# A four-layer graph network on one core: layer 0's second dense layer turned, graph 0 aggregated by rows, a bias put in PSUM by ScalarE, and other numbers for the planner

## The chip, the core and the metric

The kernel runs on one core of one Trainium2 chip. The metric is device time in microseconds for one execution on all 32 graphs. TensorE (PE in the profile) multiplies matrices and writes to the accumulator memory PSUM (8 banks of 512 fp32 columns on 128 partitions); PEld is its loading of stationary operands. VectorE (DVE) and ScalarE (ACT) do the elementwise work, GpSimd (POOL) a few powers, and SyncE (SP) issues every DMA. All data are fp32.

## The reference, cut to what matters

For each of 32 graphs there are 512 nodes with 256 features, `x`, and a dense 512 x 512 adjacency `adj`. Four layers run one after the other; each ends in a layer norm without affine.

```
layer 0: h = (1 + eps) * x + adj @ x;  x = LN(x + relu(h @ W1 + b1) @ W2 + b2)       (W1: 256x512, W2: 512x256)
layer 1: h = adj @ (x @ W.T + b);      x = LN(x + where(h > 0, h, alpha * h))        (W: 256x256)
layer 2: n = LN(x) * gamma + beta;     x = LN(x + x + relu((adj @ n) @ W_rel + b_rel + n @ W_root))
layer 3: h = (epsilon * x + adj @ x) @ W1 + b1;  h = silu(rmsnorm(h) * w)
         x = LN(x + h @ W2 + b2)                                                     (W1: 256x1024, W2: 1024x256)
```

Layer 1's bias goes through the aggregation, so in the kernel it becomes `b_1` times the row sum of the adjacency for each node.

## The kernel before, in words

**Tiling.** `x` of a graph lies in one tile of 128 partitions x 1024 columns (four chunks of 128 nodes, 256 features each), called a room; there are 36 rooms of that size. The adjacency comes as four chunks of 128 x 512, with rows and columns exchanged, in two rooms. An aggregate gives `aT`, features on partitions, nodes in columns (2 x 512).

**Seven products.** Nearly every matrix product is done as 2 x 2 blocks with seven products instead of eight (`seven`, line 800): sums of blocks are made on DVE (`left_sums`, `right_sums`), seven products go to three PSUM banks, and each result is copied (`take`) or added (`put`) to its block. An aggregate (`aggregate`, line 916) has 7 x 2 matmuls of 256 columns. To add the self-loop `1 + eps` or `epsilon`, the diagonal blocks of the adjacency and of two of its sums get a multiple of the identity (`with_loops`); layer 0 keeps the old diagonals in DRAM (graph 0: in a room) and `restore` (line 887) brings them back for layer 1.

**Dense layers.** `dense_feat` (line 956) gives its result with features on partitions and 256 columns to a matmul. The second dense layers come in two forms. `dense_add` (line 1009) has features of the tokens as output: for each product and each 128-row piece of the contraction two matmuls of 128 columns, and DVE adds each of seven results to `x` directly. `dense_turned` (line 1034) exchanges the operands: one matmul of 256 columns in place of two of 128; the results lie features first, so that ACT evicts four of them with the bias per partition, DVE adds three, DVE transposes 32 x 32 squares (two instructions), four DMAs put the squares into a DRAM tile `corner`, one DMA reads it back (`spread_squares`, line 1214), and `add_turned` (line 1073) adds the result to `x` in two halves. `TURN` (line 119) says for which graphs a layer is turned: `TURN[layer][0] < graph < B - TURN[layer][1]`. Before, only layer 3 is turned, for graphs 1 to 28. Where layer 0 isn't, `plus_row` adds its bias `b2_0` to `x` (two DVE instructions).

**Layer 1.** `dense_tok` (line 944) computes a half (256 nodes x 256 features) with four matmuls in one PSUM bank. Lines 1319 to 1327: DVE adds bias times row sum out of PSUM into `v` (two instructions a half), ACT makes `relu(-v)`, DVE the rest.

**Norms.** `Norm.half` sums each chunk and its squares on ACT (an activation and a read of its accumulator each); POOL raises the variance to -0.5; `put` (line 1149 ff.) scales a chunk on DVE or ACT, whichever the planner takes. The last two graphs (`HALVES`) are normed in two halves, with statistics on DVE, and go out by half.

**The order of the work.** The whole program is first recorded as operations with their inputs and outputs, each with a cost in microseconds for each engine that can do it. `Plan.order` (line 443) then plays them through a model of the five engines, DMA included, and writes the order out; the hardware runs exactly that order on each engine's queue. Up to 5 graphs are in flight. An operation's rank is its due time: `graph * period + need`, with `RULES` = (period, pace, spacing of the last three graphs, near) and `SHIFT` moving single graphs. `YIELD` is a penalty in microseconds for giving DVE a step that ACT can do as well. `wire_time`, `ADVANCE`, `AFTER`, `SPARE` and `KEEP` model transfers. Line 337 is a helper that issues every recorded instruction, so nearly all rows of the profile have that line and are told apart by their tiles: `ps` is PSUM, `room` a working tile, `few` small columns, `A` the sums of weight blocks, `L_gnn_W` a weight (digits left out).

**Start.** Nine warm-up matmuls on zeros (line 1405) run while the first graph is loaded; then layer 0 of graph 0 makes the sums of the adjacency, copies four diagonals on ACT, adds the loops and aggregates by seven products.

Of the kernel before, what the change touches and what calls it, by code (L numbers as in the profile page):

```python
# [14 lines left out]
P = 128  # L15
# [16 lines left out]
def matmul_time(n):  # L32
    return (0.224 if n <= 128 else 0.432), 0.163
# [34 lines left out]
ISSUE, ADVANCE, AFTER, LANES = dict(sync=0.48, within=0.66, gpsimd=1.5), 1.5, 0.4, 8  # L68
# [3 lines left out]
SPARE = 1.0  # L72
# [3 lines left out]
def wire_time(kbytes):  # L76
    return kbytes / 385


# [20 lines left out]
YIELD = 1.6  # L100
# [8 lines left out]
RULES = [(34, 1.8, 11, 0.4)]  # L109
# [3 lines left out]
SHIFT = {-1: -21, 1: 3, 2: 6}  # L113


AHEAD, LAST = 85.0, 500.0


TURN = {0: (99, 0), 2: (99, 0), 3: (0, 3)}
HALVES = 2  # L120


class Pool:
# [7 lines left out]
    def clear(self):  # L131
        self.halves = [None] * (2 * len(self.tiles))

# [18 lines left out]
    def take(self, room):  # L152
        whole, halves = self.free()
        if room.whole or not halves or whole and whole[0][0] < halves[0][0] - 1.0:
            room.index = whole[0][1]
        else:
            room.index = halves[0][1]
# [4 lines left out]
class Room:  # L162
# [3 lines left out]
    def __init__(self, pool, whole=True):  # L166
        self.pool, self.whole = pool, whole
# [65 lines left out]
class Op:  # L233
# [8 lines left out]
    kbytes: float  # L242
# [9 lines left out]
class Plan:  # L252
# [29 lines left out]
    def add(self, ways, out, ins, ordered=None, port=False, kbytes=0, late=0.0, crosses=False):  # L282
        me = len(self.ops)
        op = Op(self.graph, ways, port, crosses, "scalar" in ways, kbytes, late)
# [28 lines left out]
    def do(self, out, *ways, ordered=None, scrap=None):  # L313


        ins = []
# [29 lines left out]

    def row(self, steps):
# [21 lines left out]
    def move(self, out, src, kbytes, engine="sync", late=0.0, into=None, outof=(), issue=None, **kw):  # L369


        within = engine == "sync" and isinstance(out, Part) and isinstance(src, Part)
        kind = "within" if within else engine

        def put():
# [4 lines left out]
            {engine: ((issue or ISSUE[kind], ADVANCE + late + wire_time(kbytes) + AFTER + KEEP), put)},  # L380
            into or out, [*outof, *([src] if isinstance(src, Part) else [])],
            kbytes=kbytes, late=late,
# [60 lines left out]
    def order(self, period, pace, last, near):  # L443
# [28 lines left out]
        while can_start:  # L472
# [19 lines left out]
            def rooms_free(op):  # L492
# [7 lines left out]
                for r in first:  # L500
# [6 lines left out]
                    if not r.whole and k < len(halves):  # L507
                        taken[pool, False] = k + 1
                        at = max(at, halves[k][0])
                        continue  # L510
                    n = taken.get((pool, True), 0)
# [11 lines left out]
            for i in can_start:  # L523
# [7 lines left out]
                if op.kbytes and "sync" in op.ways:  # L531
                    wait = max(wait, lanes[0])
# [4 lines left out]
                    at, key=lambda e: at[e] + sum(op.ways[e][0]) + YIELD * (op.yields and e == "vector")  # L537
# [31 lines left out]
            if op.kbytes:  # L569
                wire = max(wire, t + ADVANCE) + wire_time(op.kbytes)  # L570
                end = wire + op.late + AFTER + SPARE
# [928 lines left out]
```

## Time and profile before

| what | us |
|---|---|
| median of 3 runs (lowest, highest) | 2285.55 (2285.33, 2286.13) |
| the profiled execution | 2285.65 |
| its span, first to last instruction | 2283.9 |
| first matmul on data / end of the last matmul | 9.59 / 2272.8 |

The mean granted TensorE clock is 0.999. The chain of work that ended last goes, in its last part, over ScalarE's rows at 2273.37 and 2277.90. Groups of instructions that the change touches, over the whole run:

| engine | what | count | mean ns |
|---|---|---|---|
| PE | matmul records, stationary `room`, moving `A`, 128 columns | 1728 | 275 |
| PE | matmul records, stationary `room`, moving `L_gnn_W`, 128 columns | 1280 | 275 |
| DVE | `room <- ps, room`, 256 columns | 944 | 416 |
| ACT | `room <- ps, L_gnn_b_c`, 256 columns (eviction with bias) | 880 | 469 |
| DVE | `room <- L_gnn_b, few, ps`, 256 columns (layer 1's bias) | 128 | 472 |
| DVE | `room <- room, L_gnn_b`, 512 columns (`plus_row`) | 72 | 686 |
| SP | `corner <- room`, 128 KB, issue to landing 2.6 us | 232 | |
| SP | `room <- corner`, 512 KB, issue to landing 3.7 us | 28 | |

How to read it: a row of the timeline has start, length, engine, line, operation, tiles written and read, shape and count, and in brackets the idle time before it with what ended it. A row of windows has the stretch, then each engine's busy time with its number of instructions, then the granted clock, the busy share of the DMA engines and GB/s. An fp32 matmul leaves two records. A record's length includes the pipeline, so that neighbours overlap: what a matmul costs in a full stream is the distance between starts.

### The profile page before, as it was taken

The numbers are of one execution on the slowest core, as the hardware profiler recorded it, in microseconds if no ns is written. First come the engines' busy times: TensorE is split into PE (matmuls) and PEld (weight loads), VectorE is DVE, ScalarE is ACT, GpSimd is POOL, SyncE is SP. The second block draws the span as 40 slices with busy tenths as digits, with TensorE's granted clock in tenths as the row PEclk, the third lists the DMA queues.
The fourth block names the chain that finished last, engine by engine and source line by source line (L and its number), as shares of the span: only waits on it lengthen the run. The fifth ranks groups of instructions, "written<-read, shape, count | busy, mean of one in ns | idle before, by whom it ended". The sixth has DMA issues, their size and how long they took to land. (4 is left out here: it accounts for less than half of the span.)

```text
span 2283.9 us, 38000 instructions
## 1 busy us (share of the span) xinstructions
PE 2268.7 (99%) x12434; PEld 2044.5 (90%) x12434; DVE 2132.9 (93%) x5471; ACT 1693.8 (74%) x4551; POOL 241.1 (11%) x168
## 2 busy tenths in 40 slices
PE   9999999999999999999999999999999999999998
PEld 8999998999988999889999899998899988988987
DVE  8999999999999999999999999999999999989898
ACT  4776677777787777777777877778777777778686
POOL 0001110111101111101111011110111101101010
PEclk9999999999999999999999999999999999999999
DMA  7102122323222232222222232322223232232201
GB/s 245 27 21 70 46 66 57 93 74 89 70 63 77 74 93 66 83 56 84 84 74 77 54 91 77 83 73 65 77 75 93 65 84 56 75 79 59 68 10 65
DMA packets 244582, 167.71 MB, mean 73 GB/s; under 512 B 141856, under 2 KB 207648, under 8 KB 244384
## 3 DMA queue, kind: packets, MB, share of 16 engines
q1 hardware_dynamic: 244384, 165.29, 25.7%
q8 instruction: 98, 1.61, 0.3%
q14 instruction: 100, 0.82, 0.1%
HBM read 109.33 MB, written 55.37 MB: 72 GB/s over the span
## 5 line engine op out<-in xcount | busy, mean ns | idle before, releaser
L337 PE MATMUL ps<-room,room 128*128 128x256 f32 x3584 | 940.9, 380 | 1.6 <-DMA room<-in_x_dram 1.2
L337 DVE TENSOR_TENSOR room<-room,room 128x512 f32<-128x512 f32 (+1 forms) x1416 | 811.6, 598 | 6.5 <-ACT room L337 1.4
L337 PEld LDWEIGHTS ps<-room,room 128*128 128x128 f32 x3584 | 651.1, 190 | 77.8 <-DVE room L337 1.8
L337 PE MATMUL ps<-room,L_gnn_W 128*128 128x256 f32 x2432 | 654.4, 380 | 1.4 <-DVE room L337 1.1
L337 DVE TENSOR_TENSOR room<-ps,room 128x256 f32<-128x256 f32 (+1 forms) x1232 | 568.2, 479 | 85.2 <-PE ps L337 78.2
L337 PE MATMUL ps<-room,A 128*128 128x256 f32 x1824 | 509.2, 380 | 0.0
L337 PEld LDWEIGHTS ps<-room,L_gnn_W 128*128 128x128 f32 x2432 | 444.4, 190 | 54.2 <-DVE room L337 1.9
L337 ACT ACTIVATE room<-ps,L_gnn_b_c 128x256 f32<-128x256 f32 x880 | 364.6, 469 | 161.4 <-PE ps L337 161.0
L337 POOL TENSOR_TENSOR few<-few,mhalf 128x4 f32<-128x4 f32 (+3 forms) x162 | 240.4, 1486 | 2035.0 <-DVE few L337 1786.0
L337 ACT ACTIVATE room<-room,few 128x256 f32<-128x256 f32 x635 | 335.0, 591 | 60.8 <-DVE few L337 60.6
L337 PEld LDWEIGHTS ps<-room,A 128*128 128x128 f32 x1824 | 326.1, 191 | 35.4 <-ACT room L337 0.9
L337 PE MATMUL ps<-L_gnn_W,room 128*128 128x128 f32 (+1 forms) x1792 | 344.4, 305 | 0.0
L337 ACT ACTIVATE scrap<-room,few 128x256 f32<-128x256 f32 x500 | 250.6, 502 | 107.8 <-DVE few L337 106.7
L337 PEld LDWEIGHTS ps<-L_gnn_W,room 128*128 128x128 f32 x1792 | 291.2, 191 | 28.4
L337 DVE TENSOR_TENSOR room<-room 128x256 f32<-128x256 f32 (+1 forms) x640 | 307.7, 495 | 4.4 <-ACT room L337 1.9
L337 ACT ACTIVATE room<-ps 128x256 f32<-128x256 f32 (+1 forms) x516 | 194.2, 378 | 153.5 <-PE ps L337 147.4
L337 PEld LDWEIGHTS ps<-A,room 128*128 128x128 f32 x1728 | 258.8, 191 | 17.7
L337 PE MATMUL ps<-A,room 128*128 128x128 f32 x1728 | 272.8, 275 | 0.0
L337 ACT ACTIVATE room<-room 128x1024 f32<-128x1024 f32 (+2 forms) x260 | 243.5, 939 | 28.1 <-DVE room L337 20.3
L337 ACT ACTIVATE scrap<-room 128x256 f32<-128x256 f32 x500 | 204.7, 412 | 51.4 <-DVE room L337 44.7
L337 ACT ACTIVATE room<-room,L_gnn_rms_weight_c 128x512 f32<-128x512 f32 x256 | 176.4, 719 | 22.0 <-DVE room L337 18.9
L337 DVE TENSOR_TENSOR room<-room,loop 128x256 f32<-128x256 f32 x256 | 105.6, 415 | 7.4 <-PE ps L337 6.5
(60 smaller groups left out, 1163.3 us busy)
## 6 DMA issues: line engine op xcount, KB each, us to landing
room<-in_adj_dram SPq DMA_DIRECT2D x128, 256.0 KB, 5.0
corner<-room SPq DMA_DIRECT2D x232, 128.0 KB, 2.6
room<-in_x_dram SPq DMA_DIRECT2D x31, 512.0 KB, 6.4
room<-corner SPq DMA_DIRECT2D x120, 128.0 KB, 2.7
out_dram<-room SPq DMA_DIRECT2D x30, 512.0 KB, 3.0
room<-corner SPq DMA_DIRECT2D x28, 512.0 KB, 3.7
diagonal<-room SPq DMA_DIRECT2D x62, 128.0 KB, 1.8
room<-in_adj_dram SPq DMA_DIRECT2D x124, 64.0 KB, 2.0
```

Of the source, the lines that this page charges most:

```text
L337: getattr(getattr(self.nc, engine), method)(to, *(put(x) for x in args), **kw)
```

## The change

- `TURN[0]` goes from (99, 0) to (2, 3): layer 0's second dense layer is turned for graphs 3 to 28; `b2c_0` is added by ACT's eviction instead of `plus_row`.
- `aggregate_first` is new, for layer 0 of graph 0: no sums of blocks, but plain rows. As each chunk of the adjacency is there, its diagonal block gets the loop and two matmuls of 512 columns add up in two full PSUM banks; the diagonal is then read again from the input. The block sums are made afterwards, for the later layers. The four diagonal copies and their moves back go.
- In layer 1 ACT writes `b_1` times the row sum into the PSUM bank, after the whole of `aT` is there (`behind=[aT]`), and all matmuls of that half add to it (none is marked as first). Relu and the last step read PSUM. The pool of banks notes how many columns the last matmuls of a bank covered (`summed`), gives the seed a bank with all 512 covered, and prefers for other uses the bank with the fewest.
- The planner's transfer model has a pair of numbers for each kind of transfer; `ADVANCE` 1.5 to 1.0 (with `AFTER` gone), `SPARE` 1.0 to 0.8, `YIELD` 1.6 to 0.8, `RULES`, `SHIFT` and `AHEAD` have other values. `ONTO` and `PLAIN` are empty, so the code that they switch does nothing.

```diff
-ISSUE, ADVANCE, AFTER, LANES = dict(sync=0.48, within=0.66, gpsimd=1.5), 1.5, 0.4, 8
-SPARE = 1.0
+ISSUE, ADVANCE, LANES = dict(sync=0.48, within=0.66, gpsimd=1.5), 1.0, 8
+SPARE = 0.8
...
-def wire_time(kbytes):
-    return kbytes / 385
+def moving(kbytes):
+    return 0.1 + kbytes / 450, 1.0
+LOAD, LOAD_X, BLOCK = (0.76, 2.15), (1.68, 1.7), (0.31, 0.66)
+CORNER, PIECES = (0.42, 0.95), (0.54, 1.16)
+TURNED, QUARTER = (1.66, 1.02), (0.7, 0.8)
...
-YIELD = 1.6
+YIELD = 0.8
...
-RULES = [(34, 1.8, 11, 0.4)]
-SHIFT = {-1: -21, 1: 3, 2: 6}
-AHEAD, LAST = 85.0, 500.0
-TURN = {0: (99, 0), 2: (99, 0), 3: (0, 3)}
+RULES = [(35, 1.7, 14, 0.2)]
+SHIFT = {-1: -21, 1: 3, 2: 5, 5: 3, 6: -1, 11: 1, 27: 1, 29: 2, 30: -3}
+AHEAD, LAST = 89.0, 500.0
+TURN = {0:(2,3),2:(99,0),3:(0,3)}
+PLAIN = 0
+ONTO = ()
+SEED = 1
+BEHINDS = 1
...
+    def fit(self, room, whole):
+        return [w for w in whole if self.summed[w[1] // 2] >= room.onto]
...
+        if self.psum:
+            whole = self.fit(room, whole)
+            ready = [w for w in whole if w[0] <= now + 1e-9]
+            i = min(ready, key=lambda w: (self.summed[w[1] // 2], w))[1] if ready else whole[0][1]
+            room.index = i
+            self.summed[i // 2] = max(self.summed[i // 2], room.sums) if room.onto else room.sums
...
-    def dense_tok(steps, h):
-        ps = bank(HC, D)
+    def dense_tok(steps, h, start=None):
+        ps = bank(HC, D, onto=start is not None)
+        if start is not None:
+            for i in range(HC):
+                start(ps[:, i, :], h * HC + i)
...
-                    n == 0 and i == 0, n == len(steps) - 1,
+                    n == 0 and i == 0 and start is None, n == len(steps) - 1,
...
+    def aggregate_first(x, adjacency):
+        aT, ps = room(DC, N), [bank(N) for _ in range(DC)]
+        for m in range(NC):
+            chunk = adjacency.chunk(m)
+            own = chunk[:, m * P : (m + 1) * P]
+            add(own, own, loop0)
+            for k in range(DC):
+                mm(ps[k], x[:, m, k * P : (k + 1) * P], chunk, m == 0, m == NC - 1)
+            block = a["adj"][plan.graph][:, m, m * P : (m + 1) * P]
+            plan.move(own, block, BLOCK)
+        for k in range(DC):
+            for h in range(2):
+                copy(aT[:, k, h * TH : (h + 1) * TH], ps[k][:, h * TH : (h + 1) * TH])
+        adjacency.sums()
+        return aT
...
     def layer0(x, adjacency):
-        adjacency.sums()
-        adjacency.with_loops(loop0)
-        aT = aggregate(x, adjacency)
-        adjacency.restore()
+        if plan.graph:
+            adjacency.sums()
+            adjacency.keep()
+            adjacency.with_loops(loop0)
+            aT = aggregate(x, adjacency)
+            adjacency.restore()
+        else:
+            aT = aggregate_first(x, adjacency)
...
-            ps = dense_tok([(aT[:, k, :], W_1[:, k, :]) for k in range(DC)], h)
-            for i in range(HC):
-                c = h * HC + i
-                stt(v[:, c, :], b_1, rs[:, c : c + 1], ps[:, i, :], ALU.mult, ALU.add)
-            act(half(neg, h), half(v, h), AF.Relu, scale=-1.0)
+            if SEED:
+                ps = dense_tok(
+                    [(aT[:, k, :], W_1[:, k, :]) for k in range(DC)], h,
+                    lambda o, c: plan.do(o, scalar(AF.Copy, D, b_1, scale=rs[:, c : c + 1]), behind=[aT] if BEHINDS else []),
+                )
+                got = ps
...
+            act(half(neg, h), got, AF.Relu, scale=-1.0)
             stt(half(x, h), half(neg, h), nalpha, half(x, h), ALU.mult, ALU.add)
-            stt(half(v, h), half(v, h), 0.0, half(x, h), ALU.max, ALU.add)
+            stt(half(v, h), got, 0.0, half(x, h), ALU.max, ALU.add)
```

## The prediction, made before the changed kernel ran

> **What bounds the kernel now.** I read the page first, then the busy time by windows, the timeline of TensorE's records, and the two ends of the timeline.
>
> ```profile
> span 2283.9 us, 38000 instructions
> PE 2268.7 (99%) x12434; PEld 2044.5 (90%) x12434; DVE 2132.9 (93%) x5471; ACT 1693.8 (74%) x4551; POOL 241.1 (11%) x168
> ```
>
> A busy PE need not be a PE at its peak, since records overlap. So I take the distance from one record's start to the next row's start, in the steady middle:
>
> ```profile
> 1006.46 2.75 PE L337 MATMUL ps<-room,L_gnn_W 128*128 128x256 f32 x12
> 1009.05 1.03 PE L337 MATMUL ps<-room,A 128*128 128x256 f32 x4
> ...
> 1034.25 1.05 PE L337 MATMUL ps<-L_gnn_W,room 128*128 128x128 f32 x8
> 1035.14 0.60 PE L337 MATMUL ps<-room,A 128*128 128x256 f32 x2
> ```
>
> Twelve records of 256 columns take 2.59 us, 216 ns each; eight of 128 take 0.89 us, 111.4 ns as a mean over the trace. Every fp32 matmul is two such records. The program has 8,360 of the first kind after the 18 warm-up ones and 4,056 of the second: 8,360 x 0.216 + 4,056 x 0.1114 = 2,257.6 us. They run from 9.59 to 2,272.8 us, 2,263.2 us. So all idle time of TensorE in between is 5.6 us (2.0 before 25 us, 0.7 by 70 us, 2.7 after 1,890 us). Windows, columns us, PE, PEld, DVE, ACT, POOL:
>
> ```profile
> 9.00:25.00 16.00, 14.14 (x63) 11.68 (x64) 15.86 (x40) 4.70 (x12) 0.00 (x0) 1.00 0.95 308
> 350.00:1890.00 1540.00, 1540.00 (x8318) 1388.53 (x8317) 1445.91 (x3678) 1170.18 (x3148) 165.95 (x110) 1.00 0.27 76
> 2030.00:2273.00 243.00, 242.34 (x1445) 219.79 (x1443) 225.50 (x559) 171.65 (x451) 26.93 (x18) 1.00 0.16 43
> ```
>
> For 1,540 us nothing but TensorE's own work sets the time, at 94% DVE and 76% ACT. Only three things can shorten the run: fewer or cheaper matmuls, an earlier start, a shorter tail behind the last matmul. The two ends:
>
> ```profile
> 7.18 2.62 SPq L377 DMA_DIRECT2D room<-in_adj_dram  x4
> ...
> 9.59 5.42 PE L337 MATMUL ps<-room,room 128*128 128x256 f32 x24 [1.22 <-DMA room<-in_x_dram]
> 14.84 1.03 PE L337 MATMUL ps<-room,L_gnn_W 128*128 128x256 f32 x4
> 16.98 1.13 PE L337 MATMUL ps<-room,L_gnn_W 128*128 128x256 f32 x4 [1.11 <-DVE room L337]
> ```
> ```profile
> 2273.37 6.49 ACT L337 ACTIVATE room<-room,few 128x256 f32<-128x256 f32 x13
> ...
> 2274.49 5.99 SPq L377 DMA_DIRECT2D out_dram<-room  x6
> ...
> 2276.83 1.05 DVE L337 TENSOR_SCALAR room<-room,few 128x256 f32<-128x256 f32 x3
> ```
>
> At the start PE waits for x. At the end the last four graphs' 16 output rows come together; ACT scales 13 of them until 2,279.86 while DVE, given 3, is done at 2,277.88. The tail behind the last matmul is 11.1 us.
>
> **What the Trainium skill says.** "TensorE: Matmul & The Clock Gate", section "Back-to-back issue gap", gives columns / 2.4 + about 2.5 ns for a warm matmul. Two cycles a column fit the fp32 records here: 512/2.4 = 213.3, measured 216.0 (2.7 over); 256/2.4 = 106.7, measured 111.4 (4.7 over, more than the page). So two narrow records cost 6.8 ns more than a wide one. "PSUM — Partial Sum Buffer", section "The four PSUM rules", says that writes of ScalarE leave the bits alone which make a matmul add rather than overwrite; so the seed must go to a bank whose last matmuls covered all 512 columns. No trace of before shows a seed. "ScalarE: Activation LUTs", section "What ACT_TABLE_LOAD costs", adds about 93 ns for a per-partition pointer; the rows agree: 412 ns with none, 502 with one, 591 with two.
>
> **The change part by part.**
>
> *Turned layer 0, graphs 3 to 28 (26 graphs).* Out go 7 x 4 matmuls of 128 columns (56 records), in come 7 x 2 of 256 (28 records): 56 x 0.1114 - 28 x 0.216 = 0.190 us a graph, 26 x 0.190 = **4.95 us off the path**. DVE loses 7 adds of 0.416 and two bias adds of 0.686 (4.28), gains 3 adds of 0.416, two transposes of 0.698 and two adds of 0.682 (4.01): 0.27 less. ACT gains 4 evictions with bias of 0.469: 1.88. SP gains five DMAs a graph, 130 in all; four issues of this kind took 1.78 us and the read-back's 0.34, 2.1 us a graph. SP mostly waits (721 us on DVE alone), so its queue holds this. Latency: transposes 1.4, issues 2, landings 2.6 and 3.7, about 10 us before the norm; other graphs' matmuls hide it, as they hide the same path of layer 3 now (no PE idle in 1,540 us). If that cover were gone, every microsecond bared would cost 26 us.
>
> *Seed, all 32 graphs.* DVE loses 4 x 0.472 = 1.89 us a graph. ACT gains 4 copies with one pointer; into PSUM this form is not in the trace. Bounds: 0.41 (no pointer) to 0.59 (two); I take 0.50, so 2.0 us. The relu and the max-add then read PSUM at their present prices (0.62; 0.68). In steady state DVE goes from 65.7 to 63.5 us of 69.8 a graph, ACT from 53.2 to 57.1 (82%): neither passes TensorE. TensorE runs the same matmuls, but the first of each half now waits for two seeds on ACT, and each seed waits for the whole aggregate. Behind a waiting seed on ACT stand copies out of PSUM that free banks. The order has other graphs' matmuls ahead, so I price it at 0; range 0 to 0.3 us per half, 64 halves, for the slow rival; below zero it cannot be, as there is no idle to remove.
>
> *Graph 0 by rows.* 28 records of 0.216 (6.05 us) become 16 of 512 columns. That form is not in the trace: 0.429 by the page's formula (an estimate), at most 2 x 0.216; I take 0.430: 6.88, **0.83 us added**. But the first matmul needs one adjacency chunk and one x half instead of two chunks, sums and an x half which stands fifth in the queue. The warm-up records hold PE until 8.2, so the start moves from 9.59 to about 8.3, **1.3 off** (0.5 if x stays behind all four chunks in SP's order, as it lands near 8.8 now). Then aT is finished in one go and its first half is copied under the last two matmuls; of the 2.0 us idle before 25 us I take 0.7 off (bounds: 2.0 off, 1.0 added, as all copies fall due together). Four 0.42 us ACT copies and four SP moves go, four diagonal re-reads of 64 KB (2.0 us landing) and four short DVE adds come; all finish under layer 0's dense matmuls. Start together: 0.83 - 1.3 - 0.7 = **-1.2** (from -2.5 to +0.5).
>
> *Order.* New margins, shifts, last graphs spaced 14 apart instead of 11, and the penalty for giving a shared step to DVE halved to 0.8. Nothing to gain in the middle, where idle is zero. At the end, 16 rows shared evenly between ACT (0.49) and DVE (0.41) need 3.6 us, not 6.5. But the last graph's own rows wait for POOL until 2,276.7, so about 2 us is what balance alone can give; I take **-1.5** (bounds: -3.1, with the graphs also spread; +0.5). The 2.7 us of idle in the drain I leave as they are.
>
> Sum: 2285.65 (the profiled run; 2283.9 span and 1.75 around it; 0.1 over the median 2285.55) - 4.95 - 1.2 - 1.5 = **2278.0**.
>
> **The rivals.**
> - *Ends give nothing.* Start and tail come out even except the 0.83: 2285.65 - 4.95 + 0.83 = 2281.5. For it: the idle moves to the dense layer at the start, and a stagger at the end leaves one graph alone with its latencies. Against: 13 rows to 3 is a plain imbalance.
> - *Ends give all.* Start -2.0, tail -3.1, drain idle -1.5: 2285.65 - 11.55 = 2274.1.
> - *The seed stalls TensorE (slower).* Place: first matmul of each layer 1 half, behind two ACT copies. ACT's longest instruction is 1.05 us, and ACT is at 82%, so a seed may come late by part of one. Price 0.3 us: 64 x 0.3 = 19.2, so 2297.2. It decides from (7.65 + 4.6)/64 = 0.19 us a half. Against: ACT's copies feed TensorE now, and the steady windows show no wait on ACT over 0.2 us in 1,540 us; taking two DVE steps out of layer 1 also shortens its chain.
>
> **How the numbers follow.** A measurement here tells 0.2% (4.6 us) from no change, so faster means under 2281.0 and slower over 2290.1. Forecast (2275 to 2280.5): 0.60. Ends give nothing (2280.5 to 2286): 0.18, a third of it still under 2281. Ends give all: 0.14. Seed stalls: 0.08, nearly all over 2290. Faster 0.60 + 0.06 + 0.14 = 0.80, same 0.13, slower 0.07. The range 2273 to 2283 leaves out the slow case (0.08), a third of the even case (0.06) and a third of the best (0.05), and takes in both bounds of the start and the tail.
>
> **What would show it.** Right: 296 records of 256 columns and 56 of 128 per graph, still no PE idle in the middle; first real matmul near 8.3; fewer than 10 ACT rows in the last 7 us; a last matmul near 2,266.5. Wrong: waits of PE on ACT at layer 1's first matmuls; DVE waiting for the read-back of the turned result; a tail over 11 us; a 128-to-256 pitch other than 111.4 and 216.

## The result, and the profile after

| | before | changed |
|---|---|---|
| time, median (us) | 2285.77 (2285.33 to 2286.13) | 2288.89 (2286.72 to 2292.23) |
| profiled run (us), span | 2285.65, 2283.9 | 2286.78, 2285.1 |
| first real matmul, last one's end (us) | 9.59, 2272.81 | 6.89, 2276.75 |
| tail behind the last matmul (us) | 11.07 | 8.35 |
| TensorE's own work, at the pitches of the prediction (us) | 2257.6 | 2253.5 |
| TensorE's idle in between (us) | 5.6 | 16.4 |
| of it before 70, 70 to 350, 350 to 1890, after 1890 us | 2.6, 0.4, -0.2, 2.7 | 3.0, 1.1, 7.8, 4.4 |

The ratio is 1.0015, 95% interval 1.0009 to 1.0021: slower by 0.15%, where 2278.0 and 0.3% faster were forecast. Work is records times pitch (0.216 us for 256 columns, 0.1114 for 128, 0.430 for 512); idle is what is left between the first matmul and the last. Of these 20 runs each, those of the changed kernel differ by up to 5.5 us from each other, those of the kernel before by 0.8. The profiled run is one of the fastest of the changed kernel, 2.1 us under its median.

The page, and two rows of TensorE's timeline at the start:

```profile
span 2285.1 us, 36862 instructions
PE 2267.2 (99%) x11694; PEld 2012.1 (88%) x11694; DVE 2113.6 (92%) x5357; ACT 1714.3 (75%) x4653; POOL 240.6 (11%) x168
```
```profile
6.89 7.03 PE L359 MATMUL ps<-room,room 128*128 128x512 f32 x16
...
15.26 1.56 PE L359 MATMUL ps<-room,L_gnn_W 128*128 128x256 f32 x6 [0.48 <-DVE room L359]
```

740 matmul records are gone, and TensorE starts 2.7 us earlier. The tail is 2.7 us shorter. All that was lost lies between. The windows say where (stretch, then PE, PEld, DVE, ACT, POOL, granted clock, DMA share, GB/s):

```profile
350.00:1890.00 1540.00, 1535.63 (x7673) 1361.06 (x7672) 1433.82 (x3604) 1180.94 (x3222) 167.23 (x110) 1.00 0.33 91
```

In the kernel before, TensorE was busy for all of these 1,540 us; the DMA engines were busy for 0.27 of them and moved 76 GB/s, against 0.33 and 91 here. The waits in the same stretch (who waited for whom: us in total, times, longest), first before, then changed:

```profile
PEld ps L337 <- ACT room L337: 0.2, 1, 0.2
PEld ps L337 <- DVE room L337: 0.2, 1, 0.2
```
```profile
DVE room L359 <- DMA room<-corner: 10.9, 12, 1.6
PEld ps L359 <- DVE room L359: 7.5, 12, 1.6
PE ps L359 <- DVE room L359: 4.2, 5, 1.2
PEld ps L359 <- ACT room L359: 2.8, 10, 0.5
```

TensorE waits for VectorE, and VectorE waits for reads of the `corner` buffers. (PEld and PE often wait together, so their rows overlap and must not be added up.) Before, no wait of VectorE for a DMA is listed in this stretch. Two kinds of read are among the 10.9 us. One is the read-back of a turned result, a single read of 512 KB. The other is layer 2's gather: layer 2 also turns a tile by squares through a `corner` buffer, with four writes and four reads of 128 KB. VectorE's groups in the same stretch tell them apart by what they write and read (count, then busy time, mean ns, idle time before, and what ended it):

```profile
L359 DVE TENSOR_TENSOR room<-room,room 128x512 f32<-128x512 f32 (+1 forms) x1026 | 589.3, 606 | 8.2 <-DMA room<-corner 5.7 <-ACT room L359 1.2
L359 DVE TENSOR_TENSOR room<-room 128x256 f32<-128x256 f32 (+1 forms) x433 | 214.8, 502 | 26.8 <-ACT room L359 19.6 <-DMA room<-corner 5.2 <-issue 1.2
```

The first, 5.7 us, is the read-back of layer 0's turned result, which is new; the second, 5.2 us in five waits, is the gather, which the kernel before has as well. Each of the five longest waits of TensorE follows one of the gather's five by about 2 us. One such place, as the chain of waits (start, length, what):

```profile
1235.39 5.37 DMA room<-in_adj_dram
...
1240.78 6.11 DMA room<-corner
...
1246.91 0.04 DVE room L359
...
1249.00 1.14 PE ps L359 x5
```

and the same microseconds on SP's queue and on VectorE:

```profile
1234.71 0.63 SPq L406 DMA_DIRECT2D out_dram<-room  x1
1235.39 2.45 SPq L406 DMA_DIRECT2D room<-in_adj_dram  x4
1237.88 0.43 SPq L406 DMA_DIRECT2D room<-in_x_dram  x1
1238.42 2.66 SPq L406 DMA_DIRECT2D room<-corner  x4
```
```profile
1246.91 0.69 DVE L359 TENSOR_TENSOR room<-room 128x512 f32<-128x512 f32 x1 [1.07 <-DMA room<-corner]
```

The chain is to be read backwards. TensorE stands 1.13 us until 1249.00 for VectorE; VectorE stood until 1246.9 for the fourth 128 KB read of layer 2's gather of graph 17; that read was issued at 1240.78, behind the 512 KB store of graph 14 and the 1.5 MB of graph 19's `adj` and `x`, and took 6.11 us to land. Its issue was late too: the third read was issued at 1239.38, but SP issued the fourth only when the first of the four `adj` chunks had landed (1240.76, the row above it in the chain). All this time the DMA engines were busy without a pause, 1.00 of the stretch where the 1,540 us have 0.33:

```profile
1232.00:1246.00 14.00, 14.00 (x66) 12.05 (x65) 9.90 (x20) 10.95 (x28) 0.00 (x0) 1.00 1.00 263
```

Similar waits of TensorE come with every second graph: matmuls wait 0.25 us and more near 1106, 1247, 1389, 1531 and 1672 us, about 142 us apart. The page's list of DMA issues (count, KB, median us to landing) shows how unusual those 6 us are, before and changed:

```profile
room<-corner SPq DMA_DIRECT2D x120, 128.0 KB, 2.7
```
```profile
room<-corner SPq DMA_DIRECT2D x120, 128.0 KB, 3.5
```

Over all 148 `corner` reads of the kernel before, none took longer than 4.42 us; of the 174 of the changed kernel one in ten took over 7.16, the longest 8.41.

### The profile page after: what moved, and what is told of

It reads as the page before. It is cut to its first block, busy times and chain, and to the rows that moved or that the text cites. A ratio compares the mean times of both kernels' runs of the same rounds, so it can differ in the third digit from the quotient of the medians.

```text
span 2285.1 us, 36862 instructions
## 1 busy us (share of the span) xinstructions
PE 2267.2 (99%) x11694; PEld 2012.1 (88%) x11694; DVE 2113.6 (92%) x5357; ACT 1714.3 (75%) x4653; POOL 240.6 (11%) x168
## 4 chain that ended last, share of the span: by engine, by line
PE 91%; DMA 4%; DVE 3%; ACT 1%; issue 0%; SPq 0%; ACTq 0%; DVEq 0%
PE ps L359 91%; DVE room L359 3%; DMA room<-in_adj_dram 1%; DMA room<-corner 1%; ACT room L359 1%; DMA diagonal<-room 0%; ACT scrap L359 0%; DMA room<-in_x_dram 0%; SPq L406 0%; DMA L_gnn_rms_weight_c<-in_L_gnn_rms_weight_dram 0%; DVE few L359 0%; ACT ps L359 0%; DVE few L384 0%; ACTq L1574 0%; DVEq L359 0%
## 5 line engine op out<-in xcount | busy, mean ns | idle before, releaser
L359 PE MATMUL ps<-room,room 128*128 128x256 f32 (+1 forms) x3572 | 947.5, 381 | 7.0 <-DVE room L359 6.5
L359 PE MATMUL ps<-room,L_gnn_W 128*128 128x256 f32 x2848 | 781.2, 380 | 1.2 <-DVE room L359 1.2
L359 PEld LDWEIGHTS ps<-room,room 128*128 128x128 f32 x3572 | 646.9, 190 | 89.6 <-DVE room L359 10.9
L359 PEld LDWEIGHTS ps<-room,L_gnn_W 128*128 128x128 f32 x2848 | 530.4, 190 | 73.8 <-DVE room L359 3.9
L359 PEld LDWEIGHTS ps<-room,A 128*128 128x128 f32 x2136 | 402.0, 190 | 55.3 <-ACT room L359 1.1
L359 ACT ACTIVATE room<-room 128x1024 f32<-128x1024 f32 x192 | 202.6, 1056 | 52.5 <-DVE room L359 51.3
L359 PE MATMUL ps<-L_gnn_W,room 128*128 128x256 f32 (+1 forms) x960 | 199.1, 331 | 0.0
L359 PEld LDWEIGHTS ps<-A,room 128*128 128x128 f32 x1104 | 163.1, 191 | 13.0 <-DVE room L359 1.3
L359 PE MATMUL ps<-A,room 128*128 128x128 f32 x1104 | 173.3, 275 | 0.0
L359 PEld LDWEIGHTS ps<-L_gnn_W,room 128*128 128x128 f32 x960 | 155.4, 191 | 15.5 <-ACT ps L359 0.3
L359 DVE TENSOR_TENSOR room<-room,loop 128x256 f32<-128x256 f32 (+1 forms) x256 | 104.5, 419 | 13.3 <-PE ps L359 5.2
```

The lines of the kernel that those rows point to most:

```text
L359: getattr(getattr(self.nc, engine), method)(to, *(put(x) for x in args), **kw)
```

## The experiments

Times stand beside runs of the kernel before on the same chip (2285.6 to 2285.8). "Middle" is TensorE's idle from 350 to 1890 us in the profiled run; it is that of a single execution, and two executions of one kernel gave 7.8 and 10.2 (changed kernel) and 7.4 and 4.4 (apart), so differences under 3 us in it mean little.

| run | time (us) | ratio, 95% | middle |
|---|---|---|---|
| changed kernel | 2288.89 | 1.0015 (1.0009 to 1.0021) | 7.8 |
| after_again | 2289.09 | 1.0016 (1.0009 to 1.0023) | 10.2 |
| lean_two | 2288.30 | 1.0010 (1.0003 to 1.0017) | 7.4 |
| no_seed | 2287.01 | 1.0007 (1.0000 to 1.0013) | 4.4 |
| no_corner0 | 2286.84 | 1.0004 (0.9995 to 1.0013) | 3.7 |
| both_out | 2284.23 | 0.9994 (0.9986 to 1.0002) | 3.7 |
| lean_five | 2284.09 | 0.9993 (0.9984 to 1.0001) | 2.0 |
| x_last | 2286.24 | 1.0004 (0.9996 to 1.0013) | 9.2 |
| apart | 2285.29 | 0.9998 (0.9989 to 1.0006) | 7.4 |
| apart_again | 2285.20 | 0.9998 (0.9990 to 1.0006) | 4.4 |
| apart_two | 2284.19 | 0.9991 (0.9983 to 1.0000) | 5.5 |
| rows_only | 2297.39 | 1.0051 (1.0032 to 1.0069) | -0.3 |
| crowd_margin | 2298.32 | 1.0056 (1.0041 to 1.0071) | 10.4 |
| turn_only | 2302.45 | 1.0073 (1.0054 to 1.0091) | 15.2 |
| old_margin | 2309.38 | 1.0108 (1.0086 to 1.0130) | 27.0 |
| no_turn0 | 2312.52 | 1.0117 (1.0098 to 1.0135) | 6.7 |
| seed_rows | 2341.51 | 1.0243 (1.0224 to 1.0262) | 4.3 |

Two kinds of run are in it. The first eight keep the changed kernel's order of instructions to the letter and take something out of it (x_last moves one thing), so they can be compared with it directly. The others let the planner draw a new order; from rows_only on, most of their time is that order's: the planner is chaotic, and turning layer 0 or not, one line, moves its own forecast for the last matmul from 2273.2 to 2284.9 us (turn_only) or from 2264.6 to 2288.8 (no_turn0). There only the middle counts, against the idle that the plan itself has there.

**lean_two.** The loads of graphs 19 and 21 carry an eighth of their partitions.

```diff
-                plan.move(self.chunk(m), a["adj"][b][:, m, :], LOAD)
+                plan.move(self.chunk(m), a["adj"][b][:, m, :], LOAD, lean=b in (19, 21))
...
-            plan.move(x, src, LOAD_X)
+            plan.move(x, src, LOAD_X, lean=b in (19, 21))
```

> The changed kernel with its order on every engine as it is, but the loads of adjacency and x of graphs 19 and 21 carry 16 of 128 partitions (an eighth of the bytes; those two graphs compute on stale data). In the changed kernel's trace TensorE idles 1.6 us near 1247, 0.8 near 1389 (the places of graphs 19 and 21), and 0.5, 1.7 and 1.8 us at the same places of graphs 17, 23 and 25. Theory (layer 2's reads of the corner tile, queued right behind the next graph's loads, land later than the planner reckoned, and DVE waits in order): the two stalls of graphs 19 and 21 go to under 0.2 us each, their reads land in under 4.5 us instead of 7 to 8, the other three stay; about 2 us less time in all. Rival (the seed copies on ACT stall TensorE): all five stay. Rival (layer 0's own corner traffic): all five stay.

The waits near 1247 and 1389 us fell under 0.15 us; those near 1531 and 1672 stayed. The gather's reads at the two thinned places landed after 2.5 to 3.9 us, where the changed kernel took 6.1 to 8.4; at the places that were left alone they still took 5.5 to 8.0. But there was no wait at 1106 either, and new ones stood at 686, 1599 and 1885 us, so the middle hardly changed (7.4), and the time came down by 0.6 us rather than 2. It speaks for the loads at these two places, and no more.

**no_seed and no_corner0.** One leaves out the 108 ScalarE copies that put layer 1's bias into PSUM (graphs 5 to 31), the other the five transfers of layer 0's turned result (graphs 5 to 28).

```diff
-                    lambda o, c: plan.do(o, scalar(AF.Copy, D, b_1, scale=rs[:, c : c + 1]), behind=[aT] if BEHINDS else []),
+                    lambda o, c: plan.do(o, scalar(AF.Copy, D, b_1, scale=rs[:, c : c + 1]), behind=[aT] if BEHINDS else [], mute=plan.graph > 4),
```
```diff
-            plan.move(places[a], of[a * Q : (a + 1) * Q], CORNER, into=name)
-        plan.move(to.whole(N * DC), via, TURNED, outof=names)
+            plan.move(places[a], of[a * Q : (a + 1) * Q], CORNER, into=name, mute=mute)
+        plan.move(to.whole(N * DC), via, TURNED, outof=names, mute=mute)
```

> The changed kernel's order with the seed copies of graphs 5 to 31 left out (108 copies; layer 1's bias is missing there). Theory (late transfers): TensorE's idle time between 350 and 1890 us, 7.8 us in the changed kernel's trace, stays between 5 and 10, and the waits at the places of graphs 17 to 25 stay; time within 3 us of the changed kernel's 2288.9. Rival (seeds stall TensorE): idle there falls under 2 us and the time to about 2280. ACT has about 50 us less work in either case.

> The changed kernel's order with the five transfers of the turned layer 0 left out for graphs 5 to 28 (120 transfers, 24 MB; layer 0's second product of those graphs is stale data). Theory (layer 2's reads behind the loads): the larger stalls at the places of graphs 17 to 25 stay at least in part, since reads still stand behind 1.5 MB of loads, the small ones go; idle between 350 and 1890 us falls from 7.8 to 3 to 6 us, time 2283 to 2287. Rival (layer 0's own traffic is the cause): idle falls under 1 us, time about 2278 to 2280, and the spread of the runs goes back to about 1 us.

Each took about 2 us off the median and 3.4 to 4.0 us off the middle, though their intervals overlap that of the changed kernel. no_corner0 fits its theory (3 to 6 us, 2283 to 2287); no_seed's 4.4 us lie between theory (5 to 10) and rival (under 2). Waits of matmuls stayed near 1251, 1392 and 1532 us in no_seed and near 1249 and 1672 in no_corner0, all smaller. In no_corner0 the gather's reads are as late as before: 40 of its 120 take over 4.42 us, as in the changed kernel. So layer 0's transfers are not what delays them, and yet the idle time falls without them. Neither is the whole cause.

**crowd_margin and old_margin.** Two new orders with all parts of the change, each with the planner's numbers searched anew. One adds up to 2 us to the due time of a small transfer behind a backlog of others, the other goes back to the kernel before's transfer times and margin.

```diff
+                back = max(0.0, wire - t - ADVANCE)
                 wire = max(wire, t + ADVANCE) + op.wire
-                end = wire + op.late + SPARE
+                end = wire + op.late + SPARE + (CROWD * min(back, 2.0) if op.wire not in (LOAD[0], LOAD_X[0]) else 0.0)
```

> All four parts of the change, planned anew with one more term in the transfer model: a transfer that is no load and is queued behind others is due later by its backlog, up to 2.0 us (the changed kernel's trace shows 1.9 to 2.1 us for such corner reads), and with RULES, SHIFT, AHEAD and YIELD searched under that model. The planner then ends TensorE's work at 2272.9, against 2264.6 for the changed kernel and 2273.2 for the kernel before. Theory (the gain was planned out of time that transfers need): this order holds on the chip: TensorE ends 1 to 3 us after the plan's figure, against 12 us after it in the changed kernel; idle between 350 and 1890 us is near the planned 1.6; time 2282 to 2286.5, spread of the runs under 3 us instead of 5.5. Rival (seeds or layer 0's turning stall TensorE whatever the transfer model): again about 12 us over the plan, so 2293 to 2297.

> All four parts of the change with the transfer model of the kernel before (wire at 385 KB/us, 1.5 + 0.4 + 1.0 us around it), RULES, SHIFT, AHEAD and YIELD searched under it. The planner ends TensorE's work at 2274.1 (6.2 us of it idle between 350 and 1890). Theory: the order holds on the chip with most of its margin, TensorE within 3 us of the plan, time 2283 to 2288, spread under 3 us. Rival (seeds or turning stall TensorE whatever the model): 2294 or more.

Both miss. Their plans had their last matmul at 2272.9 and 2274.1 us; it ended at 2287.1 and 2297.5, 14 and 23 us late. The changed kernel's ended 12 us late in the profile after and 18 in after_again (planned 2264.6), the kernel before's 0.4 us early (planned 2273.2). So a later planned end and wider margins were not enough: these orders with all parts fell behind whichever transfer times they were drawn with.

**turn_only, no_turn0, rows_only, seed_rows.** The parts one at a time, each in a new order.

```diff
-TURN = {0: (99, 0), 2: (99, 0), 3: (0, 3)}
+TURN = {0: (2, 3), 2: (99, 0), 3: (0, 3)}
```

That is turn_only, on the kernel before. no_turn0 is the changed kernel with `TURN[0]` back at (99, 0). rows_only and seed_rows have before's transfer times and rules and no turned layer 0; rows_only has no seed either.

> The kernel before with layer 0's second dense layer turned for graphs 3 to 28 and nothing else of the change; before's transfer times and rules, so the planner draws a new and worse order: its own last matmul is due at 2284.9 us, with 10.9 us of planned idle between 350 and 1890 us. Theory (turning layer 0 is what makes transfers meet and land late): the last matmul ends 6 to 14 us after the plan's, the span is 2300 to 2310, and VectorE waits for reads of the corner buffers in the middle for over 6 us in all. Rival (the turn is harmless; the seed or the fitted times do it): the last matmul is within 3 us of the plan's, as it is in the kernel before (0.4 us ahead), the span 2292 to 2299, waits on corner reads under 3 us.

> The changed kernel with layer 0's second dense layer not turned; the seed by ScalarE, graph 0 by rows, fitted times and new rules stay. The planner draws a new order whose last matmul is due at 2288.8 us. Theory (the turn does it): the last matmul within 3 us of the plan's, span 2296 to 2301, VectorE's waits on corner reads in the middle under 3 us. Rival (seed or fitted times do it): 6 us or more behind the plan, span over 2303, with waits of TensorE on ScalarE's seed of over 4 us in all.

> Graph 0 aggregated by rows with before's transfer times and rules; no turn of layer 0, no seed. The planner draws a new order, its last matmul due at 2282.6 us. Both theories: within 3 us of the plan's, span 2290 to 2296, hardly a wait of VectorE on corner reads in the middle: the control for how far an order of this kind runs from its plan. If it too is 6 us or more behind, the lateness belongs to any order but before's own.

> rows_only with the seed by ScalarE added, before's transfer times and rules, layer 0 not turned. The planner draws a new order with 0.1 us of idle between 350 and 1890 us and much idle before 350 us (last matmul due at 2331.2 us, so its whole time says nothing; the middle is what counts). Theory (the seed alone makes waits in a tight order): idle in the middle 2 to 6 us, as against none in rows_only. Rival (only the turn does): under 1 us.

Idle in the middle against that of the plan: rows_only -0.3 (planned 0), turn_only 15.2 (planned 10.9), no_turn0 6.7 (planned 0), seed_rows 4.3 (planned 0.1). By rows costs the middle nothing: no wait of TensorE is listed there. As the control it just misses its bounds: it ended 3.3 us behind its plan where at most 3 were expected, with a span of 2296.9 where 2296 was the upper end. turn_only has more waits of VectorE for reads of `corner` buffers than any other of the four:

```profile
DVE room L337 <- DMA room<-corner: 15.4, 23, 1.9
PEld ps L337 <- ACT room L337: 12.9, 29, 0.9
```

Its last matmul ended 7.8 us behind its plan, as the theory has it. no_turn0's expectation fails: 12.4 us behind, with no layer 0 turned, of which 6.7 in the middle; VectorE waits 3.7 us for reads of `corner` buffers there (under 3 expected), which without a turned layer 0 are those of layers 2 and 3. So the turn isn't needed for such waits. And seed_rows has 4.3 us of idle in the middle, with no wait of a matmul over 0.15 us; those listed are of weight loads:

```profile
PEld ps L367 <- ACT room L367: 5.6, 23, 0.4
PEld ps L367 <- DVE room L367: 0.3, 1, 0.3
PEld ps L367 <- ACT ps L367: 0.2, 1, 0.2
```

TensorE hardly waits for the seed (ACT ps, 0.2 us) but for ScalarE's other products (ACT room), which rows_only doesn't show at all. So the seed seems to have a price of its own, some 4 us in this one order and execution, and it is not paid where the slow rival put it.

**x_last.** The changed order, but `x` of ten graphs is issued behind the gather's four reads.

```diff
+            if reads:
+                done.insert(reads[-1], done.pop(i))
```

> The order of the changed kernel is kept, but the 512 KB load of x of ten graphs (5, 7, 11, 17, 19, 21, 23, 25, 27, 28) is issued after the four reads of layer 2's gather of the graph two before, in place of just ahead of them. Nothing is left out. Theory (late transfers: the gather's reads stand behind about 1.5 MB of loads): those reads land 1.5 to 2 us sooner, the waits of TensorE at 1247, 1389, 1531 and 1672 us go or fall under 0.3 us, idle between 350 and 1890 us falls from 7.8 to 3 to 5.5 us, and the time is 2284.5 to 2287.5. Rival (the order as a whole is late, loads or not; or the waits move to the later x): idle in the middle stays at 7 to 9 us and the time at 2288 to 2290.

SP's queue shows the new order:

```profile
1236.51 2.40 SPq L406 DMA_DIRECT2D room<-in_adj_dram  x4
1239.07 1.98 SPq L406 DMA_DIRECT2D room<-corner  x4
1242.56 0.35 SPq L406 DMA_DIRECT2D room<-in_x_dram  x1
```

The result is mixed. Counted from the first of the four `adj` issues ahead of it, the gather's last read landed 1.2 to 1.7 us sooner than in the changed kernel at four of the ten places, two of them those of the waits near 1389 and 1672 us, and no matmul waits there over 0.15 us any more. At the other six it landed within 0.5 us of the changed kernel's, and the waits near 1247 and 1531 stayed. At 1239 us the four reads took 7.5 to 8.0 us, since the `adj` chunks ahead of them now landed 1.1 to 1.3 us apart (0.6 to 0.8 in the changed kernel); why they did isn't shown. VectorE also waited for `adj` chunks, 5.6 us in the middle, where no such wait is listed in the changed kernel, and the middle is 9.2, at the top of what the rival has (7 to 9). The profile is of one of its longer executions (2289.19 us); the median, 2286.24, lies where the theory put it, with an interval that overlaps the changed kernel's.

So a place further ahead in the queue helped at some places and not at others. The Trainium skill, "DMA: Bandwidth & Descriptors", section "Issuing engines are not separate DMA queues", has it that all transfers run on the same 16 DMA engines and interleave there; the busy share of 1.00 around this place fits that, while of several issuers no run here tells anything, as SyncE issues them all. Its section "Two DMAs through the same engine are not ordered" adds that within one queue of an engine descriptors start in order but overlap. That agrees with the runs, which go further: in none of the profiles did a transfer (908 to 1,038 in each) land before one that was issued ahead of it.

**both_out, lean_five, after_again.** The deciding group, all in the changed order. both_out joins no_seed and no_corner0. lean_five thins out the loads:

```diff
-                plan.move(self.chunk(m), a["adj"][b][:, m, :], LOAD)
+                plan.move(self.chunk(m), a["adj"][b][:, m, :], LOAD, lean=b in (17, 19, 21, 23, 25))
...
-            plan.move(x, src, LOAD_X)
+            plan.move(x, src, LOAD_X, lean=4 < b < 29)
```

> The changed kernel in its own order, with both suspects left out for graphs 5 to 28 and 5 to 31: layer 0's five transfers for the turned result, and the ScalarE copies of the seed. Theory (several small latenesses add: turned transfers about 4 us, seed about 3.5 us of idle between 350 and 1890 us): that idle falls from 7.8 to 0 to 2 us, near the planned 0.4, and the time is 2281 to 2285.5. Rival (each omission only shifts the waits elsewhere): idle in the middle stays at 3 to 5 us, time 2285.5 to 2288.

> The changed kernel in its own order; the loads of x of graphs 5 to 28 and of adj of graphs 17, 19, 21, 23 and 25 carry 16 of 128 partitions (the rest of those buffers is what stood there). Theory (the stalls come from transfers that share the DMA engines with these loads): no wait of TensorE over 0.2 us within 4 us of 1106, 1247, 1389, 1531 and 1672 us, idle between 350 and 1890 us falls from 7.8 to 1 to 4 us, time 2282 to 2286. Rival (the order is late whatever the loads): idle in the middle 5 to 9 us, time 2286.5 to 2290.

> The changed kernel once more, as the control for how far its waits differ from one execution to the next: both theories 2286.5 to 2292, idle between 350 and 1890 us 6 to 10 us.

after_again repeats the result, with waits over 0.35 us near the same five places and a middle just over its range (10.2, at most 10 expected). lean_five has every instruction of the changed kernel, seed and turn too, and all five places are clean; one wait of a matmul over 0.15 us is left in 1,540 us. Its windows row, its waits in the middle and VectorE's group for the read-back there:

```profile
350.00:1890.00 1540.00, 1539.85 (x7710) 1367.19 (x7709) 1438.53 (x3621) 1185.25 (x3233) 167.43 (x110) 1.00 0.29 81
```
```profile
DVE room L359 <- DMA room<-corner: 6.6, 6, 2.1
PEld ps L359 <- ACT room L359: 2.5, 9, 0.6
PEld ps L359 <- DVE room L359: 1.2, 5, 0.4
```
```profile
L359 DVE TENSOR_TENSOR room<-room,room 128x512 f32<-128x512 f32 (+1 forms) x1029 | 589.8, 605 | 9.0 <-DMA room<-corner 6.6 <-ACT room L359 1.2
```

The gather's four reads near 1240 us, in the changed kernel and here:

```profile
DMA to landing us min/median/max: 6.1/7.1/7.2
```
```profile
DMA to landing us min/median/max: 2.6/2.8/2.9
```

PEld's waits for VectorE fall from 7.5 us to 1.2, PE's from 4.2 to none listed, and the median by 4.8 us, to 2284.09. The intervals of lean_five and of the changed kernel do not meet. VectorE still stands 6.6 us for reads of `corner` buffers, but now nearly all of it is the read-back of layer 0's turned result, and TensorE hardly notices: its idle time is 2.0 us.

both_out is as fast, with an interval that doesn't meet the changed kernel's either, but its middle is 3.7, not under 2, and a wait near 1106 stays (0.49 us). Its gather reads are no sooner than the changed kernel's: 40 of 120 take over 4.42 us. So there are two ways to most of the time: make these reads land sooner, or take work out of the order that they hold up.

**apart, apart_again, apart_two.** The changed kernel with nothing left out and not a line of the computation altered: only the planner's numbers, chosen so that small transfers are issued less often while loads are under way (by the planner's reckoning they stand behind others for 121 and 112 us, against 224). This is apart:

```diff
-YIELD = 0.8
+YIELD = 0.7
-RULES = [(35, 1.7, 14, 0.2)]
+RULES = [(35, 1.7, 16, 0.2)]
-SHIFT = {-1: -21, 1: 3, 2: 5, 5: 3, 6: -1, 11: 1, 27: 1, 29: 2, 30: -3}
+SHIFT = {-1: -24, 1: 6, 2: 4, 5: 1, 6: -1, 11: -2, 27: -1, 29: -2, 30: -8, 4: -1, 31: -8, 3: 3, 15: -2, 7: -2, 12: -1, 28: -1}
-AHEAD, LAST = 89.0, 500.0
+AHEAD, LAST = 107.0, 500.0
```

apart_two is drawn the same way, with `RULES` (36, 1.7, 18, 0.2), `AHEAD` 86 and other shifts.

> The changed kernel with all its parts and other numbers for the planner alone (RULES, SHIFT, AHEAD, YIELD), chosen so that fewer small transfers are issued while loads are under way: by the planner's own reckoning the small transfers stand behind 121 us of others in all, against 224 us in the changed kernel. Nothing is left out. The plan's last matmul is due at 2268.0 us, 3.4 us later than the changed kernel's. Theory (transfers that meet make the order late): the last matmul ends 3 to 8 us behind its plan, as against 12; idle between 350 and 1890 us 2 to 5 us, time 2280 to 2286. Rival (any order with all parts runs 12 us or more late): last matmul after 2279 us, idle in the middle 7 us or more, time 2288 to 2294.

> A second order drawn as in apart, with all parts and nothing left out: small transfers stand behind 112 us of others by the planner's reckoning (apart 121, the changed kernel 224); the plan's last matmul is due at 2269.7 us with 2.8 us of planned idle between 350 and 1890 us. Theory (transfers that meet make the order late): last matmul 3 to 9 us behind its plan, time 2281 to 2287, again under the changed kernel's. Rival (apart was luck): 12 us or more behind, time 2289 to 2294.

> apart once more, whose profiled execution was among the slower ones of that kernel (span 2286.1 us at a median time of 2285.29). Theory: time 2284 to 2286.5, idle between 350 and 1890 us 3 to 6.5 us. Rival: 2287 and over, idle in the middle over 7 us.

The times fit the theory: apart 3.6 us faster than the changed kernel, apart_two 4.7 us, with intervals clear of the changed kernel's. Their last matmuls end 9.0 and 5.9 (apart, twice) and 3.9 us (apart_two) behind the plan, as against 12 and 18 of the changed kernel; their plans are 3.4 and 5.1 us longer. apart's own first profile missed its end (9.0, expected 3 to 8) and its middle (7.4, expected 2 to 5); the second has 5.9 and 4.4. A longer plan alone doesn't explain the gain, as crowd_margin's is 8.3 us longer than the changed kernel's and ended 14 us late. One corner read in ten took over 4.4 us in apart_two (7.2 in the changed kernel), and VectorE waits for them 2.7 us in the middle in place of 10.9; what TensorE still waits for there is as much ScalarE as VectorE:

```profile
PEld ps L359 <- ACT room L359: 5.3, 10, 1.5
DVE room L359 <- DMA room<-corner: 2.7, 4, 1.1
PEld ps L359 <- DVE room L359: 2.2, 8, 0.5
```

apart_two is the fastest full version of this study: 2284.19 us, 1.4 us or 0.09% under the kernel before, with an interval (0.9983 to 1.0000) that just reaches it.

## Why the prediction was wrong

Against the profiled run of before, by the terms of the sum:

| term | predicted | measured |
|---|---|---|
| turned layer 0, graph 0's records | -4.95 + 0.83 | -4.1 |
| first real matmul | -1.3 | -2.7 |
| idle before 70 us | -0.7 | +0.4 |
| idle 70 to 350 us | 0 | +0.7 |
| idle 350 to 1890 us | 0 | +8.0 |
| idle after 1890 us | 0 | +1.7 |
| tail | -1.5 | -2.7 |
| sum | -7.6 | +1.2 (the spans: 2285.1 - 2283.9; the rounded rows give 1.3) |

- **Records: right.** 2,600 narrow, 9,060 wide and 16 of 512 columns make 2253.5 us, 4.1 less.
- **Start: right in kind, twice the size.** The first matmul no longer waits for `x` but comes right behind the warm-up records, as forecast. These were done by 6.89 us rather than 8.2, so it came at 6.89, not 8.3. Their end differs between executions: in the eight profiles of the changed order the first matmul came between 6.67 and 8.08 us, mostly near 7. I had taken the late end in a single trace as fixed. The 0.7 us of idle that I took off did not come: 0.48 us stand at 15.26 alone.
- **Tail: right in kind and within its bounds, more than was priced, and the reason only a third of it.** I put it down to a better balance of the last output rows, with fewer than ten on ScalarE. ScalarE still scales eleven, in 5.51 us in place of 6.49 for thirteen; that is 1.0 of the 2.7 us. Another 0.9 come from an earlier start: it begins them 0.3 us before the last matmul ends, where before it began 0.6 us after. The remaining 0.9 lie behind its last row:

```profile
2276.43 5.51 ACT L359 ACTIVATE room<-room,few 128x256 f32<-128x256 f32 x11 [1.37 <-DVE few L359]
```

- **The failed step is the zero for the middle.** I took it twice. Of the turned layer's latency, with landings of 2.6 and 3.7 us, I wrote "other graphs' matmuls hide it, as they hide the same path of layer 3 now (no PE idle in 1,540 us)", and of the new order "Nothing to gain in the middle, where idle is zero". The middle lost 8.0 us. For the turned layer's own path the cover mostly held: in lean_five VectorE stands 6.6 us for reads of `corner` buffers, nearly all for that read-back, while TensorE's idle is 2.0. What I had no term for is what the new traffic and the new order do to other transfers. I took the landing times of the kernel before as fixed, though the change adds 130 transfers and 27 MB (165 to 192 MB in SP's queue), and the new order puts layer 2's gather beside the loads: its reads, which had landed within 4.3 us, now take up to 8.4. And I took "no idle" for "there is room", though a profile without waits does not say how near the next one is.
- **That loads beside the gather make its reads late is shown; what a late read costs hangs on the rest of the order.** With the loads thin (lean_two, lean_five) the reads land after 2.4 to 3.9 us at the thinned places near these waits, and in lean_five the middle goes from 7.8 to 2.0 us and the time to 2284.1. With all the work in and fewer meetings by the planner's reckoning (apart, apart_two) the time falls by 3.6 and 4.7 us, so the order that the planner's numbers gave was itself worth that much. But in both_out, with the reads as late as ever, the time is as good as in lean_five, and without layer 0's transfers alone, or the seed alone, about half of the idle goes. The parts do not add up (both_out 3.7), since what each takes out also moves all the others in time.
- **The seed at 0 was probably mis-sized, and its rival put it in the wrong place.** The copy costs 472 ns, within my bounds (412 to 591). Listed waits of TensorE on it came to 0.3 us in the whole changed run, not to 0.3 a half. But with it the middle has more idle, with waits for ScalarE's other products: some 4 us in seed_rows against rows_only, 3.4 in the changed order (no_seed). Both rest on single executions, and no_seed's time isn't clear of the changed kernel's.
- **Of what I named as signs that I was wrong,** VectorE waiting for the read-back of the turned result came true: at 1234.05 us it stood 1.45 us for it. Waits of TensorE on ScalarE at layer 1 and a long tail did not.

What stays open: how much of the lateness of the orders in crowd_margin, old_margin and no_turn0 is transfers and how much is ScalarE and VectorE in order, since their middles hold both; and why leaving out layer 0's transfers helps although the gather's reads stay late. And of the 7.6 us that I forecast as a gain apart_two brings 1.4: its records, start and tail give about what the changed kernel's do, but 5.5 us of idle remain in its middle (2.8 of them planned), and TensorE's waits there are for ScalarE (5.3 + 1.0 us) more than for VectorE (2.2 + 1.1).

## What to carry to other kernels

Before pricing added transfers at "hidden", list what else is in flight on the DMA engines when they run, and count the reads that an in-order engine consumes within a few microseconds of landing: it is their landing time that changes, not only that of the new ones. A profile with no wait in it gives no slack; ask what the shortest distance from a landing to its reader is, and take it from the trace. Where an order is drawn by a planner, compare the planned end with the measured one for the kernel before and after: 0.4 us early against 12 to 18 us late told more than the time did, and in the orders tried here drawing for fewer meetings helped where wider margins did not.

## What the runs showed of the hardware

- In each profile all transfers of the one queue landed in the order of their issue (908 to 1,038 of them, no exception). 128 KB reads behind a 512 KB store and 1.5 MB of loads took 6.1 to 7.2 us near 1240 us, and 2.6 to 2.9 us with those loads cut to an eighth (lean_five).
- Put ahead of one 512 KB load, still behind 1 MB of others, such reads took 7.5 to 8.0 us at the same place, but landed 1.2 to 1.7 us sooner at four of ten places (x_last).
- Runs of the changed kernel scatter by 5.5 us (20 runs) and 8.2 us (18 runs, after_again), of apart_two by 2.7 us, of the kernel before by 0.8 us (20 runs) and 2.8 us (25 runs, beside apart_two). That crowded transfers make the scatter isn't shown: lean_five's runs, with the loads thin, differ by 4.4 us.
- The warm-up records start 0.43 us apart and later 0.22; where they change over differs between executions, so that all 18 are done between 6.8 and 8.4 us.
- A matmul record of 512 columns took 0.43 us (sixteen from 6.89 us to the next row at 13.76), twice one of 256 columns.
